# Routing first, no half sums on GpSimd, first matrices of both lanes ahead of the second: three moves in a four-layer gated cross-attention kernel

## The chip, the cores and the metric

The kernel runs on one core of a Trainium2 chip. The metric is the device time of one execution in microseconds; the figure quoted for a kernel is the median of its runs. Beside it stands one profiled execution, from which all durations of single instructions come.

Engine names are those of the profile: PE is TensorE (matrix products and transposes), PEld its weight loads, DVE is VectorE, ACT is ScalarE, POOL is GpSimd, and SP is SyncE, whose only work here is to issue DMAs.

## The reference

The input x has 16 sequences of 128 tokens with 256 features; a context of the same shape feeds every attention. Four layers follow, each a gated cross-attention and a gated feed-forward:

```
x = x + tanh(g_xattn[0]) * L0_xattn(q=LN(x), k=v=ctx)         # 16 heads of 16
x = x + tanh(g_ffn[0])   * L0_ffn(LN(x))                      # 8 experts, top 2, 256 -> 1024 (gelu) -> 256
x = x + tanh(g_xattn[1]) * L1_xattn(LN(x), ctx)               # softmax over the QUERIES
x = x + tanh(g_ffn[1])   * L1_ffn(LN(x))                      # linear + LoRA experts, gated by a softmax
x = x + tanh(g_xattn[2]) * L2_xattn(ctx, ctx, LN(x), mask)
x = x + tanh(g_ffn[2])   * L2_ffn(LN(x))                      # 8 swiglu experts, top 2, and a shared expert
x = x + tanh(g_xattn[3]) * L3_xattn(ctx, latents=LN(x))       # 8 heads of 64
x = x + tanh(g_ffn[3])   * L3_ffn(LN(x))                      # 8 gated experts, top 2

# L0_ffn: gate = softmax(x @ w_gate.T); the two largest experts of each token, each weighted by its gate
# L1_xattn: sm = softmax(q k / sqrt(d), axis over queries); out = sm v
```

In layer 1 the softmax is normalized over the queries. The kernel holds the scores with the keys on the partitions, so the sum for each key runs along the free axis, and its reciprocal can be multiplied into v before the second product.

## The kernel before

**Tiling.** The 16 sequences ("batches") are taken as four blocks of four batches. Everything of a token stays in SBUF; for the experts, normalized rows are scattered to a DRAM buffer `xg` in the order of their experts, read back as slots of 128 rows, and the weighted results are sent to `yd` by indirect DMAs.

**One attention step.** `attend` runs the attention of a layer as steps n = 0, 1, 2, ...: step n computes the scores of batch n (`scores`, exponentials `e` on ScalarE), the values product of batch n − 1 (`values`: ps_o, in layer 0 and 2 with the reciprocal and oT on VectorE), and the output product of batch n − 2 (`output`: ps_y, then the gated add into x on VectorE, `add_scaled`, L363). In layer 1 `scores` also sums each `e` tile (L1264 and on): for the first two of the four tiles of a batch, GpSimd first adds the two halves of the queries (`half`, L1269), and VectorE reduces the half-sized tile (L1273); for the other two VectorE reduces the whole tile. Then come the reciprocal (L1276) and the scaled v (L1278), which `values` of that batch needs.

**Side jobs.** Everything else of that stage is a generator, a job: normalizing and projecting the queries of the next block, the keys, and, `behind` each finished block, its routing (`Moe.front`). The routing normalizes the block, computes the router's logits (L418, or L426 to L437), the softmax (sm_m, sm_e, L388 and on), the two largest experts (`first_max` twice, `both` at L489), the rank of each token within its expert by two small matmuls (ps_rank, L494), the weights, and the row positions `xi` (L549), and then scatters the block's rows with eight indirect DMAs on GpSimd (L552). In layer 0, behind the routing of block 1, a plan is computed from the counts of blocks 0 and 1 (L631 to L700, `plan_i` at L698): it says which expert each of the first nine slots belongs to. A `yield` in a job ends a stage of it; `Pe(...)`, `Act(...)` or a number say on which engine the next stage begins and how it is timed.

**Who sets the order.** PE, ACT and DVE take their instructions exactly in the order in which the program emits them in `attend` (`IN_ORDER`). That order comes from a planner in the program: `Clock` gives every instruction a cost by its kind and size and keeps a time for each engine, and `poll`, `tick`, `urgent`, `until` and `idle` place a stage of a job where its inputs are due by these times. A DMA counts as done 3 us after it could begin. The order on GpSimd and on SP is left to the scheduler of the framework. All of this is fixed when the kernel is built; the chip runs one order.

**The first slots.** In layer 0 (`eager`), the slots of the plan are a job too (`filling`, `early`), taken where TensorE would be idle. `slots0` holds the weights of two experts ("lanes") at this point. Per slot it loads 128 gathered rows (`xr`, 130 KB, L782), and on a condition, where the slot begins a new expert, the first matrix (1 MB, L1577), the columns of b1, the row of b2 and the second matrix (1 MB). `near` is then 1. The order of issue is rows of slot 0, first matrix, biases and second matrix of slot 0, rows of slots 1 to 4, and then, in the loop, the first matrix of slot 1. TensorE transposes the rows (ps_xr, L815; the copy xT is on VectorE), makes the hidden layer (ps_h, L1624, 32 matmuls a slot) and, one slot later, the output (ps_e, L852, 16 matmuls a slot). From the tenth slot on there are three lanes. While those slots run, at the 24th step of their loop, the attention weights of layers 1 and 2 (`attention_weights`, L949, four loads a layer) are asked for; the scheduler of SP's queue decides where they stand.

The functions that the diff touches, and what calls them:

Of the kernel before, what the change touches and what calls it, by code (L numbers as in the profile page):

```python
# [8 lines left out]
F32 = mybir.dt.float32  # L9
# [81 lines left out]
def kernel(ctx: ExitStack, tc: tile.TileContext, a: dict, out: bass.AP):  # L91
# [349 lines left out]
    class Moe:  # L441
# [16 lines left out]
        def front(self, blk, plan=None, bias=None):  # L458


            own_set = run["fast"] and blk == NBLK - 1
            xns, xnT = yield from ln_block(blk, self.see, own_set, True)
            if bias is not None:
# [4 lines left out]
            next(soft)  # L468
            yield Act(1)
            next(soft)  # L470
# [10 lines left out]
            hot = self.kept([P, 2, BPB, NE], "hot")  # L481
            yield 1
            first_max(hot[:, 0], key, m, xns[:, :, D + 3])
            yield 1
            key2 = small("key2")
# [44 lines left out]
            )  # L530
            yield 3
            while self.passed < blk:
# [187 lines left out]
        def slots(self, n, plans, lanes, get, fetch1, fetch2, hidden, nf, far, depth):  # L720
# [151 lines left out]
            for s in range(near):  # L872
                load(s)
                first(s)
                if s < near2:
                    second(s)
# [6 lines left out]
            for s in range(n):  # L883
                while not planned(s + far + 1):
                    yield Pe(1)
                first(s + near)
                hT = yield from hidden(get, lane(s), xTs.pop(s), lambda *ps: when(s, *ps))
                if s == 0:
                    turn(1)
                turn(s + 2)  # L890
                hidden_of.append((s, hT))
                if len(hidden_of) > depth:
                    finish(*hidden_of.pop(0))
                weigh(s + 1)
                load(s + far)
                second(s + near2)
                yield Pe(0)
# [230 lines left out]
    class Fast16:  # L1128
# [86 lines left out]
        def scores(self, b, tick):  # L1215
# [45 lines left out]
            if layer == 1:  # L1261

                both = pool.tile([P, 2, H16], F32, tag="sums", name="sums")
                sums, rs = both[:, 0], both[:, 1]  # L1264
                by_pair = sums.rearrange("p (c j e) -> p j c e", c=KC, e=2)
                for j, e in enumerate(es):
                    if j < 2:
                        half = pool.tile([P, 4, S // 2], F32, tag="half", name="half")
                        nc.gpsimd.tensor_tensor(  # L1269
                            half, e[:, :, 0:S // 2], e[:, :, S // 2:], ALU.add  # L1270
                        )
                        e = half
                    nc.vector.tensor_reduce(  # L1273
                        by_pair[:, j], e.rearrange("p (c e) s -> p c e s", e=2), AX.X, ALU.add
                    )
                nc.vector.reciprocal(rs, sums)  # L1276
                self.watch.see(both.rearrange("p i h -> p (i h)"))
                nc.vector.tensor_tensor(  # L1278
                    self.spread(self.vs[b % 3]), v.rearrange("p (j e) d -> p j e d", e=2),
                    rs.rearrange("p (j e) -> p j e", e=2)[:, :, :, None].to_broadcast(  # L1280
                        [P, H16 // 2, 2, DH16]
                    ), ALU.mult,
                )
# [58 lines left out]
    class Clock:  # L1342


        def __init__(self):
            self.at = {e: 0.0 for e in (*IN_ORDER, mybir.EngineType.Pool)}
            self.done, self.read, self.rings = {}, {}, {}
            self.mode = None
            self.ends, self.moved = [], []

# [36 lines left out]
        def note(self, ins):  # L1387
# [5 lines left out]
            if "DMA" in type(ins).__name__ or ins.engine not in self.at:  # L1393
                end = max(start, self.at[PE]) + 3.0
                self.moved.append(end)
# [6 lines left out]
            for x in outs:  # L1402
                self.done[x.tensor.name] = end
            for x in srcs:
                name = x.tensor.name
# [4 lines left out]

    def attend(parts, filler=None, open_end=False, hurry=True, share=2.5, eager=False):

# [5 lines left out]

        clock = Clock()
        n = 0  # L1420
# [24 lines left out]
        def poll():  # L1445
            for job in jobs + filling:
                if job[2] is Pe:
                    continue
# [30 lines left out]
        class Tick:  # L1479
            left = 0.0  # L1480

            def __call__(self, full=True):
                if not full:
                    poll()
                    return
                end = now() + self.left
# [4 lines left out]

            def urgent(self):
                for job in jobs:
                    if job[3] and job[2] is Pe and max(job[1], bank()) <= now() + 0.1:
                        run_stage(job)
                        self.urgent()
                        return
# [24 lines left out]
        with tc.manual_schedule(engines=IN_ORDER):  # L1522
# [5 lines left out]
            for n in range(len(steps) + 2):  # L1528
# [22 lines left out]
                if n >= 2:  # L1551
                    att, b = steps[n - 2]
                    att.output(b, tick)
                    if b % BPB == BPB - 1:
                        _, _, behind, blk = blocks[(n - 2) // BPB]
                        job = begin(behind(blk), int, hurry)
                        waiting.append(job)
                        if len(waiting) <= 2:
                            jobs.append(job)
                    tick()  # L1560
# [733 lines left out]
    def layers(fast):  # L2294
# [40 lines left out]
        with tc.tile_pool(name="context", bufs=1) as cpool, ExitStack() as for_mid:  # L2335
# [16 lines left out]
            with tc.tile_pool(name="att0", bufs=2) as pool:  # L2352
# [57 lines left out]
                if fast:  # L2410
                    att = Fast16(0, pool, keys_in(pool), w, ctxT, watch)
                    attend([(att, clear, behind)], early(), eager=True)
                else:
# [235 lines left out]
```

## Time and profile before

| | |
|---|---|
| runs, median (3) | 1668.66 us (1667.05 to 1671.42) |
| profiled execution, its own time | 1609.76 us |
| its span, first to last instruction | 1607.8 us |
| mean granted TensorE clock | 0.970 |
| PE busy | 1493.5 us (93%) |
| DVE, ACT, POOL busy | 860.7, 646.7, 392.1 us |
| attention of layer 0 ends (last ps_y) | 129.05 us |
| first hidden matmul of slot 0; its second matmul | 145.24; 164.50 us |
| attention of layer 1, with its feed-forward | about 449 to 582 us |

In the lines of the profile, a TensorE row such as `145.24 6.49 PE L1624 MATMUL ps_h<-xT,w ... x32 [4.44 <-DMA w]` says: at 145.24 us from the span's start, 32 matmuls of line 1624 took 6.49 us together; before them TensorE was idle for 4.44 us, and what came last of what they waited for was the DMA that filled `w`. Groups of instructions show busy time and the mean of one in ns. A row of a stretch of time shows, in this order, its length, the busy time of PE, PEld, DVE, ACT and POOL (with the number of instructions), the granted clock of TensorE (1.00 is full speed), the mean busy share of the 16 DMA engines, and GB/s.

### The profile page before, as it was taken

Reading aid. Unit: us, or ns where it says so; the run is one execution under the profiler, and the core shown is the slowest. Engines: PE = TensorE matmul, PEld = TensorE weight load, DVE = VectorE, ACT = ScalarE, POOL = GpSimd, SP = SyncE. Lnnn points to the kernel's source line nnn. Section 1 sums busy time; section 2 is a strip of 40 time slices with the busy share of each in tenths; the row PEclk is TensorE's granted clock in tenths of the full one; section 3 lists DMA queues with packets and bytes.
Section 4 is the critical chain, followed back from the end, with each engine's and each line's share of the span. In section 5 each row is a group of like instructions: output and inputs, shape, how many; then the busy total and the mean of one; then the engine's idle time right before and its main releaser. Section 6 shows DMA issues by size and latency. Waiting matters only on the chain.

```text
span 1607.8 us, 34920 instructions
## 1 busy us (share of the span) xinstructions
PE 1493.5 (93%) x12752; PEld 1176.1 (73%) x12752; DVE 860.7 (54%) x2763; ACT 646.7 (40%) x1546; POOL 392.1 (24%) x517
## 2 busy tenths in 40 slices
PE   6994999999988999999999999999999999997992
PEld 4674889999655566665459999999965656677892
DVE  3785412223258776676345555555754437477664
ACT  5663333335546455553224333333453233224110
POOL 4234301112454322434000110111142002023531
PEclk9997999999999999999999999999999999999996
DMA  9606573534420000111064331611242000033956
GB/s 330 256 29 230 175 258 113 185 105 134 96 43 1 1 1 15 55 41 54 0 211 151 100 111 49 211 31 29 88 111 41 1 14 28 1 101 108 315 175 212
DMA packets 107768, 169.29 MB, mean 105 GB/s; under 512 B 17081, under 2 KB 77950, under 8 KB 107584
## 3 DMA queue, kind: packets, MB, share of 16 engines
q1 hardware_dynamic: 83744, 111.99, 22.1%
q0 software_dynamic: 20304, 49.66, 9.9%
q10 hardware_dynamic: 3536, 5.25, 1.0%
q8 instruction: 108, 1.77, 0.5%
q14 instruction: 76, 0.62, 0.1%
HBM read 268.42 MB, written 48.18 MB: 197 GB/s over the span
## 4 chain that ended last, share of the span: by engine, by line


## 5 line engine op out<-in xcount | busy, mean ns | idle before, releaser
L1801 PEld LDWEIGHTS ps_w<-xT,w 128*128 128x128 f32 x2304 | 264.3, 192 | 2.7 <-issue 0.4
L1801 PE MATMUL ps_w<-xT,w 128*128 128x128 f32 x2304 | 265.0, 275 | 0.2 <-issue 0.2
L864 POOL DMA_INDIRECT yd<-y,to x117 | 118.7, 1014 | 565.8 <-DVE c L827 296.8
L852 PE MATMUL ps_e<-w,hT 128*128 128x256 f32 x848 | 198.0, 380 | 2.5 <-DVE hT L1708 1.9
L852 PEld LDWEIGHTS ps_e<-w,hT 128*128 128x128 f32 x848 | 154.5, 190 | 21.6 <-DVE hT L1708 2.8
L1809 ACT ACTIVATE u<-ps_w,b 128x128 f32<-128x128 f32 x312 | 89.7, 368 | 175.8 <-PE ps_w L1801 170.7
L1624 PE MATMUL ps_h<-xT,w 128*128 128x128 f32 x1120 | 137.7, 283 | 12.4 <-DMA w<-in_l_w_dram 11.7
L1624 PEld LDWEIGHTS ps_h<-xT,w 128*128 128x128 f32 x1120 | 136.1, 200 | 15.6 <-issue 14.3
L1812 DVE SCALAR_TENSOR_TENSOR m<-ps_w,b,u 128x128 f32<-128x128 f32 x312 | 87.5, 344 | 109.1 <-PE ps_w L1801 93.8
L1629 ACT ACTIVATE hT<-ps_h,b 128x128 f32<-128x128 f32 x312 | 89.3, 373 | 119.4 <-issue 83.2
L552 POOL DMA_INDIRECT xg<-xn,xi x96 | 93.9, 978 | 108.3 <-issue 60.4
L1738 PE MATMUL ps_w<-xnT,sw 128*128 128x512 f32 x256 | 111.9, 593 | 0.0
L860 DVE SCALAR_TENSOR_TENSOR y<-ps_e,c,bias 128x256 f32<-128x256 f32 x78 | 37.6, 482 | 133.5 <-PE ps_e L852 129.7
L1110 POOL TENSOR_TENSOR sum_range<-sum_range,rs 128x256 f32<-128x256 f32 x48 | 35.4, 737 | 262.2 <-DVE rs L2218 136.3
L1738 PEld LDWEIGHTS ps_w<-xnT,sw 128*128 128x128 f32 x256 | 48.2, 190 | 56.8 <-issue 50.7
L817 DVE COPY xT<-ps_xr 128x256 f32<-128x256 f32 x117 | 48.4, 416 | 73.4 <-PE ps_xr L815 73.4
L1316 DVE RECIPROCAL rs<-ps_o 128x256 f32<-128x256 f32 x32 | 56.1, 1754 | 38.1 <-PE ps_o L1305 30.9
L1258 ACT ACTIVATE e<-ps_s 128x512 f32<-128x512 f32 x128 | 66.0, 602 | 21.8 <-PE ps_s L1243 21.8
L321 ACT ACTIVATE xn<-x,nmr,rstd 128x256 f32<-128x256 f32 x128 | 67.5, 595 | 16.3 <-DVE nmr L314 16.3
L844 ACT ACTIVATE bias<-b,c 128x256 f32<-128x256 f32 x78 | 40.3, 516 | 72.0 <-DMA b<-in_l_b_dram 28.1
L1305 PE MATMUL ps_o<-e,v 128*32 128x128 f32 x1536 | 54.3, 284 | 11.7 <-POOL sum_range L1110 4.7
L2197 ACT ACTIVATE e<-ps_s 128x512 f32<-128x512 f32 x64 | 33.4, 600 | 74.2 <-PE ps_s L2191 74.2
(273 smaller groups left out, 2578.7 us busy)
## 6 DMA issues: line engine op xcount, KB each, us to landing
w<-in_l_w_dram SPq DMA_DIRECT2D x156, 1024.0 KB
w<-in_l_w_dram SPq DMA_DIRECT2D x39, 512.0 KB
kT<-in_l_wgu_dram SPq DMA_DIRECT2D x39, 512.0 KB
xg<-zeros POOLq DMA_DIRECT2D x15, 1170.0 KB, 21.4
xr<-xg SPq DMA_DIRECT2D x78, 130.0 KB
b<-in_l_b_dram SPq DMA_DIRECT2D x78, 128.0 KB
kT<-in_l_w_dram SPq DMA_DIRECT2D x39, 256.0 KB
x<-yd POOLq DMA_DIRECT2D x48, 128.0 KB, 4.9
```

What stands on the lines that cost most here:

```text
L321: nc.scalar.activation(xns[:, i, 0:D], src, AF.Identity, bias=nmr[:, i:i + 1], scale=rstd[:, i:i + 1])
L552: self.unordered(nc.gpsimd.indirect_dma_start(out=xg[:, :], in_=xns[:, i, :], in_offset=None, out_offset=bass.IndirectOffsetOnAxis(ap=xi[: ...
L852: nc.tensor.matmul(po, lhsT=hT[:, f, :], rhs=lane(s)["w2"][:, f, :], start=(f == 0), stop=(f == nf - 1),)
L864: self.unordered(nc.gpsimd.indirect_dma_start(out=yd[:, :], in_=y, in_offset=None, out_offset=bass.IndirectOffsetOnAxis(ap=to[:, 0:1], axi ...
L1258: nc.scalar.activation(e, pss[j], AF.Exp)
L1316: nc.vector.reciprocal(rs, po[:, 1])
L1624: nc.tensor.matmul(ps[:, i, :], lhsT=w["w1"][:, k, f * P:(f + 1) * P], rhs=xT[:, k, :], start=(k == 0), stop=(k == KC - 1),)
L1629: nc.scalar.activation(hT[:, f, :], ps[:, i, :], AF.Gelu, bias=w["b1"][:, f:f + 1])
L1738: nc.tensor.matmul(ps, lhsT=wt[:, k, f * P:(f + 1) * P], rhs=xnT[:, k, :], start=(k == 0), stop=(k == KC - 1),)
L1801: nc.tensor.matmul(ps[:, f, :], lhsT=wt[:, k, s, f * P:(f + 1) * P], rhs=xT[:, k, :], start=(k == 0), stop=(k == KC - 1),)
L1809: nc.scalar.activation(u[:, f, :], pair[0][:, f, :], AF.Identity, bias=w["b1"][:, i:i + 1])
L1812: nc.vector.scalar_tensor_tensor(m1[:, f, :], pair[1][:, f, :], w["b3"][:, i:i + 1], u[:, f, :], ALU.add, ALU.mult,)
```

## The change

The change has four parts.

1. For layer 0 and blocks 0 and 1 (`express`), the routing gives up its pauses between the softmax, the two maxima and the positions, its job stands at the head of the list, and the planner takes its stages as soon as their inputs are due, also at the points within a step where it took no TensorE stage before.
2. With two lanes, the second matrix of slot 0 is asked for after the first matrix of slot 1.
3. GpSimd's half sums in layer 1 are gone; VectorE reduces all four tiles of a batch whole.
4. The planner's `Clock` for layer 0 gets a model of the loads: one queue of transfers at a fixed rate, scatters one after another on GpSimd, and no load before the plan is there. It has no instruction on the chip; it changes where the planner puts things.

No instruction is added. On PE, ACT and DVE the orders differ in two places alone: from layer 0's attention to its first slots, and in the attention of layers 1 and 2. On PE, in the order after, block 1's ps_rank stands three steps before the end of attention instead of one; the eight transposes of block 3's normalization stand before slot 0, around block 2's ps_rank (they were in the middle of slot 1), and block 3's router matmuls stand within slot 0 (they were behind slot 1); block 3's ps_rank stands before slot 0's output matmuls (it was behind slot 2's hidden ones). On DVE, block 1's positions stand behind the gated add of batch 10 instead of that of batch 12, and the plan's integers before the gated add of batch 13 instead of behind that of batch 15. On SP, three of layer 1's attention weights stood ahead of the first gathered rows; they now stand with the others, in the later loop of slots. On GpSimd, the scatters of blocks 2 and 3 stand before the first return of a slot.

```diff
@@ Moe.front
+            express = run["fast"] and self.layer == 0 and blk < NBLK // 2
             xns, xnT = yield from ln_block(blk, self.see, own_set, True)
...
             next(soft)
-            yield Act(1)
+            if not express:
+                yield Act(1)
             next(soft)
...
-            yield 1
+            if not express:
+                yield 1
             first_max(hot[:, 0], key, m, xns[:, :, D + 3])
-            yield 1
+            if not express:
+                yield 1
...
-            yield 3
+            if not express:
+                yield 3
             while self.passed < blk:
                 yield 1
@@ slots
             for s in range(near):
                 load(s)
                 first(s)
-                if s < near2:
+                if s < near2 and near > 1:
                     second(s)
...
                 first(s + near)
+                if s == 0 and near == 1:
+                    second(0)
                 hT = yield from hidden(get, lane(s), xTs.pop(s), lambda *ps: when(s, *ps))
@@ scores (layer 1)
                 for j, e in enumerate(es):
-                    if j < 2:
-                        half = pool.tile([P, 4, S // 2], F32, tag="half", name="half")
-                        nc.gpsimd.tensor_tensor(
-                            half, e[:, :, 0:S // 2], e[:, :, S // 2:], ALU.add
-                        )
-                        e = half
                     nc.vector.tensor_reduce(
                         by_pair[:, j], e.rearrange("p (c e) s -> p c e s", e=2), AX.X, ALU.add
                     )
@@ Clock.note
             if "DMA" in type(ins).__name__ or ins.engine not in self.at:
-                end = max(start, self.at[PE]) + 3.0
+                start = max(start, self.at[PE], self.plan)
+                if not self.loads:
+                    end = start + 3.0
+                elif ins.engine == mybir.EngineType.Pool:
+                    self.at[ins.engine] = max(start, self.at[ins.engine]) + 1.27
+                    end = self.at[ins.engine] + 2.5
+                else:
+                    size = self.free(outs[0]) * list(outs[0].ap)[0][1] * 4
+                    if outs[0].tensor.name in self.done and size > 2e5:
+                        size *= 0.3
+                    self.dma = max(self.dma, start) + size / 250e3
+                    end = self.dma + 2.0
...
                 self.done[x.tensor.name] = end
+                if x.tensor.name.startswith("plan_i"):
+                    self.plan = end
@@ attend
         def poll():
             for job in jobs + filling:
-                if job[2] is Pe:
+                while job[3] == 2 and job in jobs and job[2] is not Pe:
+                    queue = max(now(), clock.at[DVE if job[2] is int else ACT])
+                    if job[1] > queue + 0.3 or queue > now() + 4.0 and job[1] > now():
+                        break
+                    run_stage(job)
+                if job[2] is Pe or job[3] == 2:
                     continue
...
                 if not full:
                     poll()
+                    self.urgent(2)
                     return
...
-            def urgent(self):
+            def urgent(self, least=1):
                 for job in jobs:
-                    if job[3] and job[2] is Pe and max(job[1], bank()) <= now() + 0.1:
+                    if job[3] >= least and job[2] is Pe and max(job[1], bank()) <= now() + 0.1:
                         run_stage(job)
-                        self.urgent()
+                        self.urgent(least)
                         return
...
-                        job = begin(behind(blk), int, hurry)
+                        job = begin(behind(blk), int, 2 if blk < express else hurry)
                         waiting.append(job)
                         if len(waiting) <= 2:
-                            jobs.append(job)
+                            jobs.insert(0 if blk < express else len(jobs), job)
@@ layer 0
-                    attend([(att, clear, behind)], early(), eager=True)
+                    attend([(att, clear, behind)], early(), eager=True, express=2)
```

## The prediction

> **What bounds the kernel now.** I read the engines' shares first, then TensorE by time, then its waits, then the two places where the waits lie.
>
> ```profile
> PE 1493.5 (93%) x12752; PEld 1176.1 (73%) x12752; DVE 860.7 (54%) x2763; ACT 646.7 (40%) x1546; POOL 392.1 (24%) x517
> PE   6994999999988999999999999999999999997992
> ```
>
> TensorE is busy 93% of the span; only its 114 us of idle (1607.8 − 1493.5), and time at a low clock, can be won. The chain section of the page is empty, so the idle is located by slices. The slice row dips at the third digit (about 120 to 160 us, the end of layer 0's attention) and weakly at the 12th and 13th (layer 1's attention). Stretches of 20 us show both; the columns are PE, PEld, DVE, ACT, POOL busy, the granted clock, DMA share and GB/s:
>
> ```profile
> 120.00:140.00 20.00, 7.19 (x101) 5.14 (x93) 18.31 (x75) 5.32 (x11) 9.63 (x12) 0.85 0.33 103
> 140.00:160.00 20.00, 12.44 (x61) 11.88 (x62) 3.53 (x20) 7.58 (x20) 7.79 (x8) 0.59 1.02 346
> 440.00:460.00 20.00, 14.20 (x72) 7.80 (x76) 8.23 (x23) 11.64 (x23) 17.23 (x23) 0.95 0.69 99
> 500.00:520.00 20.00, 17.75 (x175) 11.09 (x173) 15.32 (x46) 13.73 (x32) 8.22 (x14) 1.00 0.01 2
> ```
>
> In 120–140 VectorE is full and the DMAs are mostly idle; in 140–160 it is the reverse, with TensorE at 0.59 of its clock. So the expert loads begin only when VectorE has finished. TensorE's timeline at that seam:
>
> ```profile
> 131.11 0.33 PE L434 MATMUL ps_router<-ident,logitsT 128*128 128x128 f32 x1 [0.39 <-ACT logitsT L431]
> 137.99 0.64 PE L494 MATMUL ps_rank<-both,tri 128*128 128x32 f32 x2 [6.55 <-DVE both L489]
> ...
> 140.14 0.66 PE L815 MATMUL ps_xr<-ident,xr 128*128 128x128 f32 x2 [1.09 <-DMA xr<-xg]
> 145.24 6.49 PE L1624 MATMUL ps_h<-xT,w 128*128 128x128 f32 x32 [4.44 <-DMA w<-in_l_w_dram]
> ...
> 155.16 3.75 PE L1624 MATMUL ps_h<-xT,w 128*128 128x128 f32 x16 [2.99 <-DMA w<-in_l_w_dram]
> ```
>
> Three waits in a row: 6.55 us for block 2's top-2 on VectorE, 4.44 for slot 0's first matrix, 2.99 for slot 1's. The queue that brings the matrices (SyncE) shows why:
>
> ```profile
> 134.56 0.37 SPq L949 DMA_DIRECT2D w_att<-in_l_wk_dram  x1
> ...
> 136.78 0.37 SPq L782 DMA_DIRECT2D xr<-xg  x1
> 138.10 0.38 SPq L1577 DMA_DIRECT2D w<-in_l_w_dram  x1
> ...
> 140.04 1.19 SPq L1577 DMA_DIRECT2D w<-in_l_w_dram  x1
> 141.74 2.85 SPq L782 DMA_DIRECT2D xr<-xg  x4
> 146.08 0.39 SPq L1577 DMA_DIRECT2D w<-in_l_w_dram  x1
> ```
>
> Block 1's plan is out at 134.60 and its scatters land about 135.3 (last issue 131.4, 1.27 us each, some 2.6 us to land). Then come three layer-1 attention weights (768 KB), the first gathered rows, slot 0's first matrix (used 7.1 us after its issue), slot 0's second matrix, which is not used before 164.50, and only then slot 1's first (used 9.1 us after its issue). In layer 1:
>
> ```profile
> 459.60 1.94 PE L1305 MATMUL ps_o<-e,v 128*32 128x128 f32 x32 [4.71 <-POOL sum_range L1110]
> 456.43 0.42 DVE L1273 TENSOR_REDUCE sums<-half 128x4 f32<-128x256 f32 x1 [5.09 <-POOL half L1269]
> L1273 DVE TENSOR_REDUCE sums<-e 128x4 f32<-128x512 f32 x32 | 20.3, 676 | 0.0
> L1273 DVE TENSOR_REDUCE sums<-half 128x4 f32<-128x256 f32 x32 | 13.0, 417 | 22.4 <-POOL half L1269 22.4
> ```
>
> ScalarE has the exponentials by 453.1, but GpSimd is in bias rows and accumulating DMAs until 455.13; VectorE waits 5.09 us for the half sum, and TensorE 4.71 us behind it (sum_range is only named because it ended last).
>
> **Part 1, routing of blocks 0 and 1 first.** No operation is added; they move. Block 1's rank matmul stands two batches earlier in TensorE's order (three before the tail instead of one), and its integer positions xi stand on VectorE behind batch 10's gated add, not batch 12's. Batch 12's add began at 117.77 and xi at 121.78, 4.0 us later; batch 10's began at 107.63, so xi comes at about 111.6, 10 us earlier. Eight scatters of 1.27 us follow (112.5 to 122.6) and land about 125.2; the plan has about the same time (my count of what stands ahead of it on VectorE gives 123.2). The three w_att issues move out of the queue's head to the later loop of slots near 350 us. There they add three issues (about 0.4 us each) and 768 KB, 2 us at the 380 GB/s seen at the seam. I take 0, because TensorE is full there and the DMAs are not; without that cover it is 2 us.
>
> SyncE then goes: rows(0) at 125.5, first matrix (0) at 126.8 (1.3 us later, as before), landed by 134 with the old 7.1 us; four row gathers to 132; slot 1's first matrix at 133.5, landed by 142.6 with the old 9.1; slot 0's second at about 136, landed by 145. These three are late no more.
>
> What is late next: the tail. VectorE's work behind xi sums to 19.9 us (plan 1.65 + 2.44 + 1.6, four batches of reciprocal and oT at 2.14, five of add and statistics at 1.07, smaller rest), so attention still ends near 131.5: VectorE bounds it, and no operation is saved. Block 2's logits then need thirteen small operations of 0.22 us, block 3's statistics and ScalarE's table load (1.28 us), but no more plan work (before, 133.56 to 137.93 with the plan between): rank at about 136.6, softmax tail and xi 3.1 us, the transposed rows 0.4: slot 0's matmuls begin near 140.4, where they began at 145.24. Only 5 us here.
>
> The rest comes behind it. The clock: I read 0.50 in every 2 us from 134 to 150, 0.78 in 150–152, 1.00 in 152–154, and 0.50 again in 156–160 after the 2.99 us gap. So warming took about 5.8 us from 145.24, and the short gap cost another 5.7 us at half speed. After the change: from 140.4, slot 0 (6.49 at half speed) with block 3's router inside (1.85): 5.8 us at half, then the remaining 2.5 in 1.3, to 147.6. Turn 0.4, slot 1 3.73 (warm, the form measured at 167.95), rank and turn 0.8, 1 us allowed for small waits: slot 0's second matmul at 153.5 instead of 164.50. Gain **11 us**. Block 3's normalization (1.91) now lies in the idle time ahead of slot 0. Behind 164.50 the order is the same, and the later lane waits (2.47 at 200.61, 1.79 at 234.04) follow the two-lane rhythm, so they stay. Ends: 5 (only the start moves) and 14.
>
> Queues passed: on GpSimd block 2's and 3's scatters (16 × 1.27 = 20 us) now precede the first returned slot. VectorE's y has spare buffers and TensorE does not wait on returns here; I take 0.
>
> **The clock rule.** The Trainium skill, "TensorE: Matmul & The Clock Gate", "What's actually happening", lets the clock drop after at least one idle window, about 3.4 us. By it the 2.99 us gap costs 2.99 alone, and the gain here is about 8, not 11. The row at 155.16 (16 matmuls in 3.75, as against 32 in 3.73 at 167.95) says that this gap did halve the clock; the windows run free, and earlier idle may count. I take the row.
>
> **Part 2, half sums off GpSimd.** Removed: 32 adds on GpSimd. Added: 32 reductions grow from 417 to 676 ns, 8.3 us of VectorE over 16 batches, 0.5 per batch. At 451–459: exponentials end at 453.1, four reductions at 0.6 us pitch end about 453.8, reciprocal and v 0.7 more: 454.6, ahead of the normalization's end at 454.90. The 4.71 stall goes, and with it the half-speed matmuls behind it (1.94 against 1.08, 1.91 against 1.03, 1.46 against 1.15: 2.1 us). Sum −6.8. Against it stand stalls on VectorE itself, in stretches where it is continuously busy:
>
> ```profile
> 513.00:528.00 15.00, 10.90 (x111) 7.49 (x108) 13.88 (x40) 8.83 (x20) 7.05 (x11) 0.89 0.01 2
> 522.74 1.81 PE L1305 MATMUL ps_o<-e,v 128*32 128x128 f32 x32 [3.20 <-DVE x L363]
> ```
>
> and 2.62 at 559.46, with six of 0.37 to 0.89. Each of the eight may grow by 0.5 (+4), or shrink where the half sum was the last to come (−2.4 in all). I take +0.8: **−6 us**, ends +3 and −9.
>
> **Sum.** −11 − 6 = −17 us. Behind layer 1 nothing moves and TensorE is full, so it reaches the end. The sum stands against the profiled execution, 1609.76 (span 1607.8): about 1592.8. The runs' median, 1668.66, is 58.9 us above it, which I carry over unchanged: **1651.7**.
>
> **Rivals.** (a) Only the start moves: the clock stays low longer, or slot 1 waits anyway for a matrix issued behind five row gathers. For: the DMAs ran at 340 to 409 GB/s from 146 on. Against: slot 1's matrix gets 15 us now. L0 −5, L1 −6: 1657.7. (b) VectorE takes back all of part 2: L1 0, L0 −11: 1657.7. For: 13.88 of 15 us busy above. Against: 22.4 us of its waits on half sums disappear. (c) Block 1's routing, run in one piece (some 2.5 and 3.1 us), holds up reciprocals, attention ends some 10 us later, and the start gains nothing: −6 alone, 1662.7. Against: TensorE's 4.47 us per batch leaves VectorE 1.26 over its 3.21. (d) The other side: in layer 1 the longer reductions hold v and the gated add behind the gating chain in all four blocks, 0.5 × 16 = 8 us and a new gap beyond 2.5 us per block with about 3 us of half clock each (12): +20 in place of −6, net +9: 1677.7. It decides from layer 1 losing over 16 us. Against: from 528 to 549 and from 563 to 582 TensorE is full while VectorE is busy 13.09 of 21 and 11.15 of 19 us, so the blocks have room between their crowded stretches.
>
> **Numbers.** Chances: forecast 0.60 (own range 1643 to 1660), (a) 0.15, (b) 0.10, (c) 0.08, (d) 0.07. No change means within 0.3%, 5 us, about what runs of this kernel can tell. Faster: nearly all of the first, most of (a) and (b), under half of (c), 0.83; same 0.10; slower 0.07. Range: 1642 (−14, −9 and 4 more for stalls that shrink) to 1666, which leaves out (d) and the tails.
>
> **What would show it.** Right: block 1's xi near 111.6; first slot rows issued near 125.5 with no w_att ahead; slot 0's first matmul near 140.4, waiting for VectorE, not for w; no w wait before slot 1; slot 0's second matmul near 153.5; no half rows, and no 4.7 us wait ahead of the first ps_o of layer 1; gated-add and vb waits of about 3 us still there. Wrong: the attention tail past 133; w waits at slot 0 or 1; new VectorE waits over 2.5 us in layer 1; or the lane wait at 200 growing by what was won.

## The result, and the profile after

| | before | changed |
|---|---|---|
| median (5 runs each) | 1668.97 us (1667.05 to 1673.30) | 1653.80 us (1649.46 to 1656.99) |
| ratio | | 0.9903 (0.9878 to 0.9928) |
| profiled execution's span | 1607.8 us | 1652.1 us |
| forecast | | 1651.7 (1642 to 1666) |

The median is 2 us from the forecast. The two spans do not fit: the changed kernel is faster by its runs and 44 us longer by its profile. The kernels of one set ran on one chip, and the same kernel before took 1669 us in the first sets and 1605 to 1608 in the later ones; the profile shown ahead of the prediction is of the second kind, the first profile of the changed kernel of the first. So I compare profiles of one kind: `after` with `before_again` (span 1667.0), and `after_again` (span 1597.4) with the profile of before.

The busy shares on the page of the first profile of the changed kernel:

```profile
PE 1521.3 (92%) x12752; PEld 1189.3 (72%) x12752; DVE 865.0 (52%) x2763; ACT 644.7 (39%) x1546; POOL 368.2 (22%) x485
```

TensorE is busy 28 us longer than in the profile of before, with the same instructions. Its list of waits (line, what it waited for, us in total, times, longest) has in its first and its fifth place what the profile of before hardly has (1.6 us in all):

```profile
PE ps_o L1306 <- issue: 12.5, 30, 1.0
PE ps_o L2231 <- issue: 5.7, 10, 1.1
```

"issue" names nothing that the engine waited for. Here is such a stretch in TensorE's timeline:

```profile
119.87 1.08 PE L1306 MATMUL ps_o<-e,v 128*32 128x128 f32 x32
120.77 0.40 PE L1306 MATMUL ps_o<-e,ones 128*32 128x128 f32 x8
121.42 0.39 PE L1306 MATMUL ps_o<-e,ones 128*32 128x128 f32 x2 [0.25 <-issue]
122.11 0.43 PE L1306 MATMUL ps_o<-e,ones 128*32 128x128 f32 x5 [0.30 <-issue]
...
127.22 2.07 PE L1328 MATMUL ps_y<-w_att,oT 128*128 128x256 f32 x4 [1.01 <-issue]
```

and GpSimd's timeline in the same stretch, the first and the last of eight rows:

```profile
120.11 1.06 POOL L557 DMA_INDIRECT xg<-xn,xi  x1 [4.47 <-DVE cnt L645]
...
129.06 0.96 POOL L557 DMA_INDIRECT xg<-xn,xi  x1 [0.30 <-issue]
```

Thirty-two small matmuls that take 1.06 us elsewhere are stretched over 5.4 us, a few at a time, while GpSimd issues block 1's eight scatters. Block 0's scatters do the same at 89 to 98 us. The gaps are not all of it: the other engines also learn late that TensorE is done. VectorE's next reciprocal reads the result of these matmuls:

```profile
131.74 1.76 DVE L1317 RECIPROCAL rs<-ps_o 128x256 f32<-128x256 f32 x1 [6.72 <-remote]
```

("remote": the profile finds no instruction that ended this wait.) It begins 5.5 us after the last of these matmuls has ended by the profile, and 1.7 us after the last scatter has (130.02).

Now the seam as the later profile (`after_again`) shows it, against the lines ahead of the prediction. SyncE's timeline:

```profile
124.44 0.37 SPq L787 DMA_DIRECT2D xr<-xg  x1
125.77 0.38 SPq L1599 DMA_DIRECT2D w<-in_l_w_dram  x1
...
131.69 0.38 SPq L1599 DMA_DIRECT2D w<-in_l_w_dram  x1
134.05 0.38 SPq L1599 DMA_DIRECT2D w<-in_l_w_dram  x1
```

TensorE's timeline:

```profile
136.61 0.64 PE L498 MATMUL ps_rank<-both,tri 128*128 128x32 f32 x2 [0.71 <-DVE both L493]
139.99 3.78 PE L1646 MATMUL ps_h<-xT,w 128*128 128x128 f32 x16 [0.98 <-DVE xT L822]
143.56 3.42 PE L418 MATMUL ps_router<-wgl,xnT 128*128 128x8 f32 x16
146.84 3.76 PE L1646 MATMUL ps_h<-xT,w 128*128 128x128 f32 x16
...
151.54 3.85 PE L1646 MATMUL ps_h<-xT,w 128*128 128x128 f32 x32
...
155.85 3.62 PE L857 MATMUL ps_e<-w,hT 128*128 128x256 f32 x16
```

The two 20 us stretches, with the columns as before:

```profile
120.00:140.00 20.00, 10.78 (x116) 7.41 (x115) 17.35 (x67) 8.40 (x18) 5.16 (x8) 0.86 0.68 207
140.00:160.00 20.00, 19.91 (x113) 19.10 (x114) 7.84 (x41) 9.45 (x22) 8.83 (x10) 0.71 0.61 198
```

No layer-1 weights stand ahead of the rows, there is no wait for w before slot 0 or 1, and TensorE is busy 19.91 of 20 us where it was busy 12.44. In layer 1, the wait of 4.71 us, which was to go, is there, and longer. TensorE's timeline of `after_again`:

```profile
454.11 1.93 PE L1306 MATMUL ps_o<-e,v 128*32 128x128 f32 x32 [5.59 <-DVE v L1279]
```

GpSimd's:

```profile
448.94 3.28 POOL L359 TENSOR_TENSOR x<-x,rows 128x256 f32<-128x256 f32 x4
...
451.88 1.89 POOL L359 TENSOR_TENSOR x<-x,rows 128x256 f32<-128x256 f32 x2
```

and VectorE's, with the next batch's scaling as the measure:

```profile
449.66 4.39 DVE L1279 TENSOR_TENSOR v<-vb,sums 128x256 f32<-128x256 f32 x1
...
457.15 0.43 DVE L1279 TENSOR_TENSOR v<-vb,sums 128x256 f32<-128x256 f32 x1
```

The sums are ready at 449.56, but the scaling of v takes 4.39 us instead of 0.43, and ends (454.05) just after GpSimd's run of additions does (453.77).

### The profile page after: what moved, and what is told of

Same layout as the page of the kernel before. It is cut to its first block, busy times and chain, and to the rows that moved or that the text cites. A ratio compares the mean times of both kernels' runs of the same rounds, so it can differ in the third digit from the quotient of the medians.

```text
span 1652.1 us, 34864 instructions
## 1 busy us (share of the span) xinstructions
PE 1521.3 (92%) x12752; PEld 1189.3 (72%) x12752; DVE 865.0 (52%) x2763; ACT 644.7 (39%) x1546; POOL 368.2 (22%) x485
## 4 chain that ended last, share of the span: by engine, by line
## 5 line engine op out<-in xcount | busy, mean ns | idle before, releaser
L857 PEld LDWEIGHTS ps_e<-w,hT 128*128 128x128 f32 x848 | 154.4, 190 | 22.4 <-DVE hT L1730 2.8
L1646 PE MATMUL ps_h<-xT,w 128*128 128x128 f32 x1120 | 137.3, 282 | 9.1 <-DMA w<-in_l_w_dram 4.1
L1117 POOL TENSOR_TENSOR sum_range<-sum_range,rs 128x256 f32<-128x256 f32 x48 | 35.2, 734 | 282.7 <-DVE rs L2240 143.9
L1265 ACT ACTIVATE e<-ps_s 128x512 f32<-128x512 f32 x128 | 65.9, 602 | 19.1 <-PE ps_s L1250 19.1
```

Source lines behind the costliest of these rows:

```text
L857: nc.tensor.matmul(po, lhsT=hT[:, f, :], rhs=lane(s)["w2"][:, f, :], start=(f == 0), stop=(f == nf - 1),)
L1265: nc.scalar.activation(e, pss[j], AF.Exp)
L1646: nc.tensor.matmul(ps[:, i, :], lhsT=w["w1"][:, k, f * P:(f + 1) * P], rhs=xT[:, k, :], start=(k == 0), stop=(k == KC - 1),)
```

## The experiments

Ratios are to the kernel before in the same set, with 95% intervals. A stage is read from TensorE's timeline: the last output product (ps_y) of layer 0's attention, the first hidden (ps_h) and output (ps_e) matmul of slot 0, and the first ps_v of layer 1.

### First set: kernel before at 1669.4 us

**The kernel before again** (no edit).

> The kernel before, unchanged, profiled once more on the chip where the variants run. Theory A: TensorE loses about 60 us in most executions to gaps that the profile calls issue, in which its instructions arrive a few at a time while the indirect scatters run; the profile of before that was shown happened to hold almost none (0.7 us). Then this profile has a span of 1650 to 1670 us, 15 us or more of issue gaps ahead of ps_o, and the 58.9 us between profile and median are gone. Theory B: those gaps belong to the changed order alone, and the 58.9 us lie outside the span: then the span is again 1606 to 1610 us without issue gaps, and the median 1668.

Measured: 1670.03 us, 1.0003 (0.9988 to 1.0017), span 1667.0. The 58.9 us lie inside the span, in two halves. TensorE is idle 29.4 us longer, and its issue gaps grow by 28.0 (29.6 us instead of 1.6). It is also busy 29.8 us longer (1523.3 instead of 1493.5): 94.4 us of its work fell on half clock instead of 55.4, which is worth some 20 of these. Of the gaps, 29.1 us lie within a microsecond of a packet on GpSimd's DMA queue; such stretches make up 558 of the 1667 us, so chance would give a third. Theory A's picture holds, though the gaps alone are half of its 60 us, and B's does not. In this profile block 0's scatters cost the loop 8 us (15.2 us from one output product to the next, 7.5 in the first profile). Block 1's, at 127 to 137 us, reach the loop only at its end (133.7); behind it, block 2's router waits 2.92 us for the copy of its logits, 0.39 in the first profile.

Block 0's burst has all eight scatters in twelve of the traces. In the five of this kind (`before_again`, `after` and the next three) the semaphore (a counter) by which the other engines wait for TensorE then stands still for 10.3 to 11.0 us and moves again 1.5 to 1.8 us after the last scatter. In the seven others it never stands still for more than 2.6 us there.

**No half sums alone** (part 3).

```diff
-                    if j < 2:
-                        half = pool.tile([P, 4, S // 2], F32, tag="half", name="half")
...
-                        e = half
```

> The kernel before with part 3 alone: no half sums on GpSimd. Prediction's term: -6 us (ends +3 and -9), so a median near 1663. The first ps_o of layer 1 waits no more for 4.7 us. Rival (b): VectorE takes it all back, 1669. In the profile of the changed kernel layer 1 came out about 11 us shorter (from +7.2 to -4.5 against before); if that is part 3 alone, 1658.

Measured: 1662.39 us, 0.9948 (0.9928 to 0.9968): −7 to −9 us, the forecast's term. But this trace has the long scaling of v too (3.99 us), so the gain is not from the stall that I had named. Neither this part nor the next was run alone on a chip without the gaps.

**Routing and order without part 3.**

```diff
+                    if j < 2:
+                        half = pool.tile([P, 4, S // 2], F32, tag="half", name="half")
...
+                        e = half
```

> The changed kernel with the half sums put back: parts 1, 2 and 4. Prediction's term: -11 us, median near 1658. If most of the gain is in layer 1 (as the profile of the changed kernel suggests, where slot 0's second matmul came at 169.5 against 164.5 before, with issue gaps ahead of it), the median is 1665 to 1669. With part 3 the two should add up to -15.

Measured: 1671.31 us, 1.0012 (0.9995 to 1.0029), no gain. Attention ends at 144.6 us instead of 133.7, with both bursts of scatters inside the loop (issue gaps at 91 to 99 and 124 to 129 us), slot 0 begins at 155.1 instead of 149.9, and layer 1 begins 1.5 us earlier (459.9 against 461.4). What routing wins behind the seam is paid ahead of it, and at slot 1, which waits 5.04 us for its transposed rows; `after`, with the same order there, waits 0.81. The parts do not add up to the whole here (0.9948 and 1.0012 against 0.9903); the runs of this kernel spread from 1658.5 to 1679.9, and I leave that open.

**Order of the second matrix alone** (part 2).

```diff
-                if s < near2:
+                if s < near2 and near > 1:
...
+                if s == 0 and near == 1:
+                    second(0)
```

> The kernel before with part 2 alone: slot 0's second matrix asked for after slot 1's first. The wait of 2.99 us ahead of slot 1 falls, and with it the half clock behind it (2.9 us): -3 to -6 us if the wait was due to the order, median 1663 to 1666. If the transfer is only as fast as the DMAs allow behind five row gathers, 0, and slot 0's second matrix is not late either (it has 18 us).

Measured: 1670.72 us, 1.0016 (0.9998 to 1.0034): nothing. Slot 1 waits 5.04 us, for its transposed rows (in `before_again` 3.09 us, for the same). GpSimd's timeline with the last of block 2's eight scatters, and VectorE's with the copy of these rows:

```profile
158.67 0.96 POOL L552 DMA_INDIRECT xg<-xn,xi  x1 [0.30 <-issue]
161.32 0.76 DVE L817 COPY xT<-ps_xr 128x256 f32<-128x256 f32 x2 [11.47 <-remote]
```

The copy comes 1.7 us after the scatter's end, 4.6 us after TensorE's transposes have ended by the profile. In `before_again` and in the run above, whose loads start early, it also comes 1.7 us after it (159.68 and 167.04). So on this chip slot 1 waits for the scatters and not for w, and this run cannot tell what the order of the matrices is worth where it waits for w, as in the first profile of the kernel before.

### Second set: kernel before at 1607.4 us

**The changed kernel again** (no edit).

> The changed kernel once more, on the chip of the variants beside it, for a fair comparison with them: 0.990 of before again (about 1653). If the gain of 15 us belonged to the chip or hour of its first runs, it comes out near the sum of the parts measured alone, -7 (no half sums) and 0 (routing), about 1662.

Measured: 1589.10 us, 0.9895 (0.9876 to 0.9914): −17 us by the ratio and −18 by the medians, with 1.1 us of issue gaps. The profiled execution is the slowest of the five (1599.11; the others took 1587 to 1591). Its span is only 10.4 us below that of before, so some 7 us of the gain cannot be placed in it.

**Only block 0's routing first.**

```diff
-            express = run["fast"] and self.layer == 0 and blk < NBLK // 2
+            express = run["fast"] and self.layer == 0 and blk < 1
...
-                    attend([(att, clear, behind)], early(), eager=True, express=2)
+                    attend([(att, clear, behind)], early(), eager=True, express=1)
```

> The changed kernel with only block 0's routing taken first; block 1's goes the planned way as before. Theory A (scatters starve TensorE of instructions): block 1's burst falls again behind the last values products, attention of layer 0 ends near 135 instead of 142, and slot 0 starts near 148 to 151 instead of 152.9: the time is within 4 us of the changed kernel's or better by up to 4. Theory C (the early routing itself, not the scatters, holds up the loop through VectorE): attention ends at 137 to 139, between the two.

Measured: 1594.33 us, 0.9923 (0.9904 to 0.9941). Without issue gaps on this chip it does not tell A from C. It does tell what block 1's early routing is worth where scatters cost nothing: slot 0 begins at 146.7 instead of 140.0, but its output matmuls come only 1.5 us later (157.3 against 155.8): block 3's router stands ahead of slot 0 here and not within it (see the run with this routing held back). In all it is 0.9923 against 0.9895, with intervals that overlap.

**Seven of eight scatters left out, in the kernel before and in the changed one.**

```diff
                 for j in range(2):
+                    if self.layer == 0 and blk < 2 and i + j:
+                        continue
                     self.unordered(nc.gpsimd.indirect_dma_start(
...
+                        for i in range(0, B * S, 8 * P):
+                            nc.gpsimd.dma_start(
+                                out=yd[i:i + 8 * P, :].rearrange("(p r) d -> p r d", p=P),
+                                in_=zeros[:, :, 0:D].to_broadcast([P, 8, D]),
+                            )
```

> The kernel before with seven of the eight scatters of blocks 0 and 1 in layer 0 left out (and the result rows cleared at the start by two more DMAs of 1 MB): these rows are not computed. Theory A: the 15.8 us between two output products at 88 to 104 us fall to 7 or 8, no issue gaps there, layer 0's attention ends near 126 instead of 133.7. Theory C or a stall with another cause: it still ends near 133.

> The changed kernel with the same seven of eight scatters left out in blocks 0 and 1 (and the same clearing). Theory A: both slow stretches go (12.4 and 10.6 us between output products), attention ends near 129 instead of 142.4, slot 0's second matmul comes 10 to 14 us ahead of that of the kernel before with the same scatters left out, as the prediction had it (11). Theory C: attention still ends 8 us or more behind that kernel's, and the second matmul gains 0 to 4 us.

Measured: 0.9974 (0.9961 to 0.9986) and 0.9850 (0.9829 to 0.9871). The clearing stretched one step near 50 us by some 5 us, so attention ends later (135.4 and 133.2), and neither trace had issue gaps to lose. With few scatters the changed kernel's second matmul comes 16.7 us ahead of the other's (151.4 against 168.1), so the early routing as such does not hold up the loop: that speaks against C. For A it decides nothing.

### Third set: kernel before at 1604.8 us

**Bias adds behind the scaling of v**, in the changed kernel and in the one before.

```diff
-            if self.bias is not None:
+            if self.bias is not None and layer == 1:
+                self.late.append(blk)
+            elif self.bias is not None:
                 add_bias(blk, self.bias)
...
+            while self.late:
+                for x in block(self.late.pop(0)):
+                    tc.add_manual_dep(
+                        nc.gpsimd.tensor_tensor(xs[x], xs[x], self.bias, ALU.add).ins,
+                        scaled.ins.name,
...
```

> The changed kernel with layer 1's sixteen bias adds on GpSimd (L359) held behind the scaling of v that VectorE does in the same step. In the changed kernel the first scaling of v took 4.39 us instead of 0.42, just as long as GpSimd was adding, and TensorE waited 5.59 us. Theory P (the two engines exclude each other where VectorE reads two tensors from SBUF): that scaling is 0.42 us again, the wait falls below 1.5 us and the half clock behind it goes (about 2 us): 5 to 8 us faster than the changed kernel, ratio to before near 0.985. Theory Q (v waits for something else, such as its cleared buffer or the sums): it stays at 4 us or more, no gain, ratio 0.990.

> The kernel before with the same bias adds held back and the half sums kept. If the 4.71 us wait came from GpSimd being busy with accumulating DMAs and these adds ahead of the first half sum, most of it goes: 4 to 7 us faster than before, ratio near 0.997. Then the removal of the half sums and the place of these adds are two ways to the same stall, and the gain of no half sums lies elsewhere, in the crowded stretches of VectorE. If the half sums waited for the DMAs alone, the wait stays above 3 us and the ratio is 1.000.

Measured: 1580.03 us, 0.9845 (0.9821 to 0.9870), and 1597.52 us, 0.9951 (0.9933 to 0.9968). The changed kernel's layer 1 with the adds held back, in TensorE's timeline:

```profile
444.48 1.08 PE L1318 MATMUL ps_o<-e,v 128*32 128x128 f32 x32 [0.81 <-DVE v L1281]
```

in VectorE's:

```profile
443.91 0.52 DVE L1281 TENSOR_TENSOR v<-vb,sums 128x256 f32<-128x256 f32 x1
```

and in GpSimd's, where the adds now follow:

```profile
444.57 2.94 POOL L1290 TENSOR_TENSOR x<-x,rows 128x256 f32<-128x256 f32 x4
```

Theory P holds: the scaling takes 0.52 us, the wait is 0.81 instead of 5.59, the matmul behind it is at full speed (1.08 against 1.93), and the way from layer 1's first ps_v to its third takes 8.1 us instead of 15.3. The Trainium skill has this rule ("GPSIMD Engine Reference", "Specifications": the two engines share SBUF interfaces and contend where a VectorE instruction has two SBUF inputs or runs in a two-port mode); the trace agrees with 4.39 us against 0.43 to 0.52. The reductions, with one input, kept their pace: in `after_again` six of them ran beside GpSimd's elementwise instructions, at 675 ns against 676. One input alone does not spare an instruction: the small `ve<-mv` took 1.90 us beside two of GpSimd's additions, 0.17 without. In the kernel before, the same edit took the stall from 4.71 to 2.96 us, less than I expected of it, and won 8 us in all; its profile is 3.6 us ahead already at slot 0's second matmul (160.87 against 164.50), which the edit does not touch, so how much of the 8 is the edit's own stays open. The changed kernel with this edit has the lowest time of this study.

**Block 3's routing held back behind slot 0's hidden layer.**

```diff
+            while run["fast"] and self.layer == 0 and blk == NBLK - 1 and not self.warm:
+                yield 1
             own_set = run["fast"] and blk == NBLK - 1
...
                 hT = yield from hidden(get, lane(s), xTs.pop(s), lambda *ps: when(s, *ps))
+                self.warm = True
```

> The changed kernel with block 3's routing (normalization, router, rank) held back until slot 0's hidden layer is done, so that no narrow router matmuls (128x8) stand within slot 0. Theory W (these matmuls do not count toward warming the clock): slot 0's 32 hidden matmuls run at half speed for about 5.8 us from their start and the clock is full from there, instead of 10.4 us; slot 0's second matmul comes near 151 to 152 where it was 155.8, and then 3.7 us of normalization and router at full clock follow later, so the total is within 3 us of the changed kernel, ratio 0.988 to 0.991. Theory V (the clock's windows or the idle time ahead of slot 0 set it): half speed still lasts 8 us or more from slot 0's start.

TensorE's timeline at slot 0:

```profile
140.10 5.86 PE L1650 MATMUL ps_h<-xT,w 128*128 128x128 f32 x32 [1.84 <-DVE xT L825]
...
146.70 3.84 PE L1650 MATMUL ps_h<-xT,w 128*128 128x128 f32 x32 [0.30 <-DVE xT L825]
...
150.59 3.62 PE L860 MATMUL ps_e<-w,hT 128*128 128x256 f32 x16
```

Measured: 1591.62 us, 0.9914 (0.9896 to 0.9931), no gain in all; the routing comes later instead. But slot 0's output matmuls come at 150.59 instead of 155.85. The clock's record changes in steps of 3.41 us. In `after_again` it is half from 134.5 to 151.6, and TensorE is busy almost without a break from 140: the two steps that hold router matmuls (141.4 to 148.2) did not raise it, the first that held wide matmuls alone did. Here the first such step, 141.0 to 144.4, raised it. That is theory W, and other traces agree: two steps with router matmuls in `after` (154.3 to 161.1) and one that they fill almost alone in `express_one` (139.9 to 143.3) did not raise it either.

How much of the 5 us is the router's and how much is phase, that is, where the steps happen to fall, `after_late_bias` tells. It has the router within slot 0, as `after_again` has:

```profile
141.10 3.39 PE L1658 MATMUL ps_h<-xT,w 128*128 128x128 f32 x16 [0.99 <-DVE xT L822]
144.33 1.85 PE L418 MATMUL ps_router<-wgl,xnT 128*128 128x8 f32 x16
...
153.09 3.62 PE L857 MATMUL ps_e<-w,hT 128*128 128x256 f32 x16
```

A step of wide matmuls ended at 143.9, just before the router, and raised the clock. From slot 0's start to its output matmuls it is 12.0 us, against 15.9 in `after_again` and 10.5 in this run. So 3.9 of the 5.4 us are phase, and the other 1.5 are about the router's own time at full clock (1.85).

### Fourth set: kernel before at 1608.1 us

**Scatters left out for block 1 alone** (`blk == 1` in place of `blk < 2` above).

> The changed kernel with seven of the eight scatters left out for block 1 of layer 0 alone (and the result rows cleared at the start); block 0's eight scatters stay, as the control in the same trace. Where the chip shows issue gaps at all (as in the first profile of the changed kernel: 90 to 98 and 121 to 131 us): Theory A expects block 0's gaps unchanged and none for block 1, with the attention of layer 0 ending 6 to 10 us earlier than 142.4 (the clearing may cost up to 5 of it). If the gaps of block 1 stay without its scatters, the scatters are not their cause. Where the chip shows no such gaps (as in the later profiles), there is nothing to take away, and attention ends near 133 as with both bursts left out: then the cause stays open.

Measured: 0.9858 (0.9811 to 0.9906), attention ends at 131.9. The chip showed no issue gaps, block 0's burst included, so this decides nothing. That the gaps come with the scatters is shown by their place in five profiles of the first kind. No run took scatters away where the gaps occur, but the order moved them: block 1's burst ends at 137.3 us in `before_again`, at 130.0 in `after` and at 132.1 in `routing_only`, and TensorE's semaphore stands still for 11.6 and 11.7 us around the latter two, until 1.6 and 1.8 us after their ends. That speaks for the scatters as the cause; by what path, and why one chip shows it and others do not, stays open. In `before_again`, the 16 KB packets of instructions, which I take to be TensorE's, came at 87.2 and 107.1 us and none between, so a late packet is not what block 0's gaps there wait for.

## Why the prediction was right, point by point

The total, −17, was met in both kinds of runs (ratios 0.9903 and 0.9895; −15 and −18 us by the medians). That it came so close is in part luck: of its steps, some held and three did not; the profile of `after_again` shows 10.4 us of the gain; and on the chip with the gaps the −11 of the routing, taken alone, measured 0.

- **The seam's times held, in `after_again`.** Block 1's xi came at 111.28 (111.6 forecast), the rows at 124.44 (125.5), slot 1's first matrix at 131.69 (133.5), rank at 136.61 (136.6), slot 0 at 139.99 (140.4). As forecast, slot 0 waits for VectorE and not for w, and attention ends about where it did (last output product at 129.48, before 129.05).
- **The warm-up was mis-sized.** "5.8 us at half, then the remaining 2.5 in 1.3" counted the router's matmuls as work that warms the clock. It also took two times for half-clock ones that are not: the router's 1.85 us (3.42 at half clock) and slot 0's 6.49, partly at full clock (3.78 and 3.76 at half); so it left out 1.3 us. Slot 0 with the router took 10.6 us instead of 7.2, and the second matmul came at 155.85, not 153.5: 8.7 us won, not 11. With a kinder phase, in `after_late_bias`, slot 0 with the router took 7.0 us and the second matmul came at 153.09.
- **The lane waits did not stay.** They were 2.47 and 1.79 us; they are 3.25 and 2.52, and the slot behind the last now runs at half speed too (5.44 us against 3.81). The first grew by 0.8 us, far from all that was won. Of the 8.7 us, 6.5 reach layer 1 (442.45 against 448.95).
- **Layer 1 had the right size by another way.** "The 4.71 stall goes" is the step that failed: it was priced without the competition of the two engines over SBUF, which the half sums had hidden behind another wait. The −6 came all the same, −7.2 from the start of layer 1 to the end of layer 2's attention (251.7 to 244.5), in the stretches whose term was taken as +0.8: the 3.20 us wait in the first crowded stretch is gone, and between the 8th and the 14th output product of layer 1 the lead goes from −1.2 to +5.3 us (65.9 and 127.9 after its start before, 67.1 and 122.6 now). VectorE's group of reductions in `after_again` fits that (busy us, mean ns, idle before): the 64 full ones have 5.2 us of idle ahead of them, where the half-sized ones had 22.4. No run tests this cause by itself:

```profile
L1274 DVE TENSOR_REDUCE sums<-e 128x4 f32<-128x512 f32 x64 | 39.4, 676 | 5.2 <-ACT e L1265 5.1
```

- **The 58.9 us, "which I carry over unchanged",** held as a sum and not as a reason. Both kernels carry the issue gaps where they occur. But there the changed kernel has block 1's burst inside the loop: attention ends 8.7 us later than in `before_again` (142.4 against 133.7), and slot 0's second matmul comes at the same time (169.5 against 169.6). The gain of layer 0, 4.8 us at the start of layer 1, arises behind that: 3.6 of it at one slot, which in `before_again` waits 3.46 us for w and then runs at half clock (6.43 us), and in `after` waits 2.50 us and runs at full clock (3.81). Neither rival (c), which has VectorE hold up the loop, nor any other case of mine had this; it has (c)'s outcome by another engine.
- **Rival (d)** did not come: no stall in layer 1 grew beyond 3 us in the crowded stretches (2.98 at 546.78, before 2.62).
- **The clock rule.** Waits shorter than a window can halve the clock: one of 2.43 us in the fastest kernel is followed by a slot of 5.44 us. They need not: the one of 2.50 us in `after` is followed by a slot of 3.81. So the row was the right choice for that execution, and phase decides what such a gap costs. The free-running window of about 3.4 us that the Trainium skill gives ("TensorE: Matmul & The Clock Gate", "What's actually happening") does show: half-clock stretches last 3.41, 6.83, 10.24, 13.65 or 17.07 us, but for the last of each profile.

## What to carry to other kernels

Before you move a burst of GpSimd scatters, ask what TensorE issues beside it: where many small matmuls run, the burst may cost as much as the earlier start wins, and one chip may show it where another does not. When you take work off GpSimd, look at what remains there at that moment, since its additions can hold a two-input VectorE instruction for as long as they last. Before you explain a few microseconds behind a pause of TensorE, look where the steps of its clock fell in each profile. And compare profiles only with profiles whose span stands in the same relation to their runs.

## What the runs showed of the hardware

- TensorE's small matmuls (64 per batch in `ps_o`) slowed from 1.06 us for 32 to 5.4 us while GpSimd issued indirect scatters, in the profiles of one kind; in those of the other the same program at the same place did not slow. In the first kind the engines that waited for TensorE went on 1.5 to 1.8 us after block 0's last scatter. Between the two kinds the kernel before differs by 59 us of span: 28 are issue gaps, and some 20 more work at half clock.
- A VectorE instruction with two SBUF inputs took 4.39 us instead of 0.43 beside a run of GpSimd additions; moving sixteen additions by some microseconds was worth about 8 us (0.9895 to 0.9845).
- Narrow router matmuls (128x8) kept TensorE busy for 3.42 us without raising its clock from half; a step of 3.41 us with wide matmuls raised it.
